# Source turns in halves beside the projections, and score maxima sent in groups, in a transformer block on one core

## The chip, the cores and the metric

The kernel runs on one core of a Trainium2 chip. The metric is the device time of one execution in microseconds (us). TensorE (PE, with its weight loads listed as PEld), VectorE (DVE), ScalarE (ACT) and GpSimd (POOL) compute; SyncE (SP) issues nearly all DMA transfers. Each engine works through its own instructions in order and waits for the others by semaphores.

## The reference

A diffusion-transformer block for 16 batches of 256 tokens, width 256, 16 heads of 16, all in 32-bit floats. What matters here:

```python
x_norm = modulate(_ln(x), shift_a, scale_a)
q, k, v = jnp.split(x_norm @ W_qkv + b_qkv, 3, axis=-1)          # then split into heads
attn_w = softmax(einsum('bhqd,bhkd->bhqk', q, k) * scale)
x = x + gate_a[:, None] * (einsum('bhqk,bhkd->bhqd', attn_w, v) @ W_proj + b_proj)
q_c = _ln(x) @ W_qc + b_qc
k_c, v_c = jnp.split(_ln(context) @ W_kvc + b_kvc, 2, axis=-1)
x = x + cross_attention(q_c, k_c, v_c) @ W_cproj + b_cproj
x = x + gate_m[:, None] * (gelu(modulate(_ln(x), shift_m, scale_m) @ W_mlp1 + b_mlp1) @ W_mlp2 + b_mlp2)
```

## The kernel before

**Units and beats.** The work is a sequence of 32 units, numbered n: the self-attention ("s") and the cross-attention ("c") of each batch. The first five are s units, then s and c alternate, and the last five are c units. After a prologue (n = −1) each unit is worked on in eight beats, k = 0 to 7, by `beat(n, k)`; the MLP of all batches follows. A unit has 16 heads in eight pairs, and four groups g of two pairs.

In beat k of unit n, PE does three kinds of work:

- `visit` computes the scores s of unit n+1 (query rows on partitions) for half t of the tokens of group k // 2: four matmuls into the tile `s` (two PSUM banks, one copy; `s_tile`), two on rows 0 to 63 and two on rows 64 to 127. VectorE reduces them to maxima (tile `mx`, one reduction per beat). It then computes the scores of unit n once more, transposed (`st`, `t_part`), for pair k, and ScalarE takes their exponential into `pt` (`exp`). The transposed scores have the maxima subtracted already, because row 63 of each half of the q operand (`u.q[63:P:64]`) holds minus the maximum and the matching row of k holds ones.
- In even beats `av_part` multiplies the exponentials with the values (tile `o`, in four column tiles of 32).
- In odd beats two *lanes* run side by side, one on rows 0 to 63 and one on rows 64 to 127 (`lane`, `lanes`, `run`): twelve pairs of matmuls for two of the projections Q, K, V (of units n+2 and n+3) and P (of unit n−2). A lane's product is summed over two visits, one half of the rows in each. Beat 1: Q and V; beat 3: P and Q; beat 5: K and P; beat 7: V and K. Where the unit n+3 is a c unit, two lane pairs of beat 5 run between s and st; where n > 1, the first lane pair of beat 7 runs in beat 6.

**Turns of the sources.** A projection's source is the layer-normed input `xn` (128 tokens by 256, twice), turned by PE with an identity into PSUM (`transposed.turn`: four turns of 128 × 128, tile `psT`), then copied out as a high and a low part (`high` on ScalarE, `low` on VectorE, or `full` and `rest_pool`). `T[0]` of unit n+3 is turned half in beat 0 and half in beat 2 of unit n, if it is ready; a c unit has a second source `T[1]`, turned in beat 4.

**The maxima** of a unit are turned in two halves of two groups each (`m_turn`, 16 columns), scaled by −1 on ScalarE (`m_row`, tile `m`) and copied by one DMA into row 63: groups 0 and 1 of unit n+1 in beat 4 of unit n, groups 2 and 3 in beat 0 of the unit itself. In beat 4 the turned maxima borrow a bank of `st` where n+3 is a c unit, and in beat 0 a part of the turned source's bank.

**PSUM.** `st` and `s` take two banks each, the LONG tag one (values and P), and the SHORT tag has three, shared by the tiles `ps_q`/`ps_qc`, `ps_k`/`ps_kc`, `psT`, `psm` and `o`. A new tile takes one of the three banks that has come free and its first writer waits for the last reader of the tile before. The last readers are: for Q and K the low part on VectorE (`l_q` in beat 4, `l_k` in beat 0 of the next unit, both after that beat's reduction), for `o` the copy to `oT` on ScalarE (beat 5, and beat 0 of the next unit), for a turned source its low part (or the copy `y_c`) in beat 3, for `T[1]` its low part in beat 7.

**Order.** The program order on each engine is that of the calls (`tc.keep_in_program_order`). In beat 0 that is: K's high part on ScalarE, s, st, exponential, `o` of the unit before and its copy, turns, maxima, K's low part. Helper calls are all listed at line 51.

Of the kernel before, what the change touches and what calls it, by code (L numbers as in the profile page):

```python
# [21 lines left out]
def pixart_block(  # L22
# [354 lines left out]
    def transposed(src, name, scale=None, pool=False):  # L377
# [6 lines left out]
        def turn(fs=range(KC)):  # L384
            if len(fs) == KC:
                place()
            for f in fs:
                for t in range(NT):
                    PE.transpose(o.ps[:, f * N + t * P:f * N + (t + 1) * P],
                                 src()[:, t, f * P:(f + 1) * P], ident)  # L390

        def high():
# [78 lines left out]
    def lanes(x, y):  # L471


        if x:
            x.ps, x.fresh = ps_gen(f"ps_{x.name}", LONG if x.tok else SHORT), True
        return zip_longest(*(lane(o, half) for half, o in enumerate((x, y)) if o))

# [4 lines left out]
    def to_stack(W, src, bias, dst, which, name):  # L482
# [24 lines left out]
        def low():  # L507
# [3 lines left out]
            if name == "k0":  # L511
                gap(work, 192, "gap_mx")
            for f in range(KC):
# [65 lines left out]
    def build_pre(u):  # L579

        b = u.b
        u.mx = None
        if u.kind == "s":
# [111 lines left out]
    turn_of_s = [0]  # L695

    def s_tile(u, g, par, t, bank=None, home=sp):

# [7 lines left out]
        for j in range(2):  # L706
# [3 lines left out]
            if j == 0:  # L710
                yield
        if u.mx is None:
            u.mx = work.tile([P, 2, 2, 4, NT], F32, tag="mx", name=f"mx_{u.n}", bufs=3)
        mx = u.mx.rearrange("p f r a t -> p r f a t")
        a = slice(2 * (g % 2), 2 * (g % 2) + 2)
        if alone or apart:
            src = home[bank] if apart else sp[:, bank]
            DVE.tensor_reduce(mx[:, par, g // 2, a, t], src.rearrange("p (j n) -> p j n", j=2),
                              AX.X, ALU.max)
# [8 lines left out]
    def m_turn(u, hf, pst=None):  # L728

        if pst is None:  # L730
            pst = ps_gen(f"psm_{u.n}_{hf}", SHORT)
        PE.transpose(pst[:16, :P], u.mx[:, hf].rearrange("p r a t -> p (r a t)"), ident)
        return pst

    def m_row(u, hf, pst):

        m = work.tile([16, P], F32R, tag="m", name=f"m_{u.n}_{hf}", bufs=1)
        ACT.mul(m, pst[:16, :P], -1.0)
        SP.dma_start(u.q[63:P:64, 4 * hf:4 * hf + 4, :].bitcast(F32), m.bitcast(F32))

# [23 lines left out]

    def in_turn(*pieces):

        for _ in range(2):
            for f in pieces:
                next(f)

    def av_part(u, g):

        if g % 2 == 0:
            u.po = ps_gen(f"o_{u.n}_{g}", SHORT).rearrange("p (g n) -> p g n", g=2)
        for c in range(NT):
            for h in range(4):
# [301 lines left out]

    def visit(n, k, home=sp, between=None):

# [8 lines left out]
        t = [t_part(units[n], k, par) for par in range(2)]  # L1089
        in_turn(*s)  # L1090
        if between:
            between()
        in_turn(*t)
        later.append(lambda: exp(units[n], k))

    def spare(n, gate=True):
# [6 lines left out]
    def beat(n, k):  # L1103
# [20 lines left out]
        if k == 6:  # L1124
            if q2 and not n:
                q2.V.keep()
            if p2 and not alone:
                p2.end()
        kp = None
        if k == 5 and lx and n:  # L1130
            kp = lanes(q3.K, None if alone else p2)
        visit(n, k, between=kp and (lambda: run(kp, 2)))
        if k == 0:
            exps()
            if prev:
# [17 lines left out]
        elif k == 1:  # L1153
            exps()
            run(lanes(q2 and q2.Q, q2 and n and q2.V))
            if prev:
# [8 lines left out]
        elif k == 2:  # L1165
            exps()
            if cur:
                av_part(cur, 0)
            if q3:
                q3.T[0].turn((1,) if q3.ready else (0, 1))  # L1170
            if ls:
# [26 lines left out]
        elif k == 4:  # L1198
# [20 lines left out]
        elif k == 5:  # L1219
            exps()  # L1220
            run(kp or lanes(q3 and q3.K, (None if alone else p2) if n else q2.V))
            if cur:
# [10 lines left out]
        elif k == 6:  # L1233
# [139 lines left out]
```

## Time and profile before

| | |
|---|---|
| median of 3 runs | 719.96 us (719.1 to 720.77) |
| profiled execution, from its first to its last instruction | 719.7 us |
| PE busy | 710.4 us (99%), 8993 matmuls |
| DVE busy | 567.8 us (79%), 895 instructions |
| ACT busy | 551.7 us (77%), 955 instructions |
| POOL busy | 520.6 us (72%), 518 instructions |
| reductions of the maxima (units −1 to 30) | start from 21.4 us on (the four into `st` from 19.4), the last at 519.1 us |

An instruction is listed as `out<-in`, by the program's tile names without buffer numbers, with its shape. A busy PE isn't PE at its peak: matmuls are pipelined and their ends are modelled, so a wait of its weight loads may lie under a matmul that is still listed as running. In a timeline, the columns are start, duration (both in us), engine, line, operation, output and inputs, shape and count; a bracket tells how long the engine was idle before it and what ended that.

### The profile page before, as it was taken

Reading aid. Unit: us, or ns where it says so; the run is one execution under the profiler, and the core shown is the slowest. Engines: PE = TensorE matmul, PEld = TensorE weight load, DVE = VectorE, ACT = ScalarE, POOL = GpSimd, SP = SyncE. Lnnn points to the kernel's source line nnn. Section 1 sums busy time; section 2 is a strip of 40 time slices with the busy share of each in tenths; the row PEclk is TensorE's granted clock in tenths of the full one; section 3 lists DMA queues with packets and bytes.
Section 4 is the critical chain, followed back from the end, with each engine's and each line's share of the span. In section 5 each row is a group of like instructions: output and inputs, shape, how many; then the busy total and the mean of one; then the engine's idle time right before and its main releaser. Section 6 shows DMA issues by size and latency. Waiting matters only on the chain.

```text
span 719.7 us, 22488 instructions
## 1 busy us (share of the span) xinstructions
PE 710.4 (99%) x8993; PEld 592.3 (82%) x8993; DVE 567.8 (79%) x895; ACT 551.7 (77%) x955; POOL 520.6 (72%) x518
## 2 busy tenths in 40 slices
PE   9999999999999999999999999999999999999997
PEld 8777777777877778777787777777779999999997
DVE  5878888888888798888888888888675777777653
ACT  5677888888888788887888888887867677666661
POOL 7655778787776867776686798977857988656651
PEclk9999999999999999999999999999999999999999
DMA  7574455554545456454655656456323132313212
GB/s 236 183 233 157 160 170 178 175 179 160 167 151 196 162 176 191 163 166 153 195 167 176 210 174 195 156 192 196 95 78 103 59 87 61 88 46 88 66 39 74
DMA packets 81548, 106.15 MB, mean 147 GB/s; under 512 B 16610, under 2 KB 44548, under 8 KB 81444
## 3 DMA queue, kind: packets, MB, share of 16 engines
q1 hardware_dynamic: 80548, 104.37, 45.5%
q8 instruction: 71, 1.16, 0.7%
q10 hardware_dynamic: 896, 0.35, 0.2%
q14 instruction: 33, 0.27, 0.1%
HBM read 35.89 MB, written 8.98 MB: 62 GB/s over the span
## 4 chain that ended last, share of the span: by engine, by line
PE 94%; DVE 3%; POOL 2%; issue 0%; ACT 0%; POOLq 0%; ACTq 0%
PE s L51 18%; PE o L51 16%; PE st L51 16%; PE ph L51 12%; PE ps_qc L51 4%; PE ps_kc L51 4%; PE ps_k L51 4%; PE ps_q L51 3%; PE ps_v_c L51 3%; PE ps_v_s L51 3%; PE ps_P_s L51 2%; DVE mx L51 2%; PE ps_P_c L51 2%; PE psT_c L51 2%; PE psT_s L51 2%; PE psT_q L51 1%
## 5 line engine op out<-in xcount | busy, mean ns | idle before, releaser
L51 DVE TENSOR_REDUCE mx<-s 128x4 f32<-128x1024 f32 x252 | 307.9, 1222 | 73.5 <-PE s L51 70.1
L51 ACT ACTIVATE pt<-st 128x1024 f32<-128x1024 f32 x256 | 263.4, 1029 | 51.8 <-PE st L51 51.0
L51 PE MATMUL o<-pt,v 128*32 128x256 f32 x2048 | 137.1, 385 | 0.0
L51 PE MATMUL s<-big 63*128 63x256 f32 x1008 | 116.8, 305 | 1.7 <-DVE st_q L51 0.8
L51 PE MATMUL st<-big 64*128 64x256 f32 (+1 forms) x1040 | 107.7, 282 | 0.8 <-issue 0.4
L51 PE MATMUL ph<-xTh_m,wself 128*128 128x256 f32 x512 | 100.2, 281 | 0.0
L51 POOL TENSOR_TENSOR hl<-hf,hh 128x512 fp32r<-128x512 f32 x60 | 80.1, 1350 | 20.8 <-ACT hh L51 20.8
L51 PEld LDWEIGHTS s<-big 63*128 63x128 f32 x1008 | 77.3, 185 | 21.0 <-issue 7.1
L51 PEld LDWEIGHTS o<-pt,v 128*32 128x32 f32 x2048 | 53.4, 109 | 39.5 <-ACT oT L51 1.3
L51 PEld LDWEIGHTS st<-big 64*128 64x128 f32 (+1 forms) x1040 | 81.2, 186 | 3.6 <-ACT pt L51 1.5
L51 PEld LDWEIGHTS ph<-xTh_m,wself 128*128 128x128 f32 x512 | 82.3, 188 | 1.2 <-issue 0.4
L51 PE MATMUL ph<-xTl_m,wself 128*128 128x256 f32 x256 | 71.1, 278 | 0.0
L51 ACT ACTIVATE hf<-ph,bT 128x256 f32<-128x256 f32 x112 | 47.0, 473 | 22.1 <-PE ph L51 21.9
L51 ACT ACTIVATE hh<-ph,bT 128x256 fp32r<-128x256 f32 x112 | 47.0, 472 | 19.8 <-PE st L51 8.4
L51 PEld LDWEIGHTS ph<-xTl_m,wself 128*128 128x128 f32 x256 | 48.2, 188 | 0.0
L51 PE MATMUL s<-big,hh 128*128 128x256 f32 x256 | 45.6, 278 | 0.0
L51 DVE TENSOR_SCALAR xn_m<-x,mv_m,rs_m 128x256 f32<-128x256 f32 x28 | 33.5, 1237 | 14.8 <-POOL rs_m L51 14.8
L51 POOL TENSOR_SCALAR xn_q<-x,mv_q,rs_q 128x256 f32<-128x256 f32 x32 | 38.9, 1225 | 1.7
L51 POOL TENSOR_SCALAR xn_c<-c,mv_c,rs_c 128x256 f32<-128x256 f32 x32 | 38.9, 1226 | 1.7
L51 PE MATMUL st<-big,hh 128*128 128x256 f32 x224 | 40.0, 278 | 0.0
L51 PEld LDWEIGHTS s<-big,hh 128*128 128x128 f32 x256 | 38.8, 188 | 0.0
L51 POOL TENSOR_SCALAR rs_c<-mv_c 128x2 f32<-128x2 f32 x16 | 3.6, 228 | 48.3 <-DVE mv_c L51 48.2
(230 smaller groups left out, 2133.1 us busy)
## 6 DMA issues: line engine op xcount, KB each, us to landing
big<-h_k SPq DMA_DIRECT2D x32, 256.0 KB
big<-h_kc SPq DMA_DIRECT2D x32, 256.0 KB
big<-h_qc SPq DMA_DIRECT2D x32, 256.0 KB
big<-h_q SPq DMA_DIRECT2D x30, 256.0 KB
big<-l_k SPq DMA_DIRECT2D x16, 256.0 KB
g<-gd SPq DMA_DIRECT2D x16, 256.0 KB
U_s<-oT SPq DMA_DIRECT2D x32, 128.0 KB
R_s<-rd_s SPq DMA_DIRECT2D x16, 256.0 KB
```

The costliest lines, as they stand in the source:

```text
L51: i = f(*a, **k)
```

## The change

The turn of a source is split into two halves by rows (`half(h)`: rows 64h to 64h + 63, four turns of 64 × 128 into 64 columns each). In beat 1 (`T[0]` of unit n+3, if ready) and beat 5 (`T[1]`, for c units) a new PSUM tile is taken for the source after that of Q or K, and the first half runs between the first and the second pair of the score matmuls (`mid`), mixed with two matmuls of the second lane in the order t, b, t, t, b, t (`turning`). The lanes of that beat then run ten pairs, and the last two matmuls of the first lane run in the next beat (2 or 6), between s and st, mixed with the second half of the turn. The turns of beats 0, 2 and 4 go, as do the two lane pairs between s and st in beat 5. Where n+3 is a c unit, the lane pair of beat 6 goes back to beat 7.

The maxima have a constant tile of four places (`mxs`), each with two groups of eight columns. In beat 2, ahead of the matmuls of `o`, one place is turned by two plain matmuls with the identity in column tiles of 32 (`m_cols`): group 3 of unit n and group 0 of unit n+1. In beat 6 another follows: groups 1 and 2 of unit n+1. They are written to the free half of the bank of `o`, scaled on ScalarE and sent by four DMAs (`m_send`). The turns of the maxima in beats 0 and 4 go (but for unit 0).

```diff
+    mxs = const.tile([P, 4, 32], F32, name="mxs")
+    POOL.memset(mxs, 0.0)
+    mxs = [mxs[:, i] for i in range(4)]
...
+        def half(h):
+            rows = slice(64 * h, 64 * h + 64)
+            for f in range(KC):
+                for t in range(NT):
+                    c = f * N + t * P + 64 * h
+                    PE.transpose(o.ps[:, c:c + 64], src()[rows, t, f * P:(f + 1) * P], ident[rows, rows])
+                    yield
...
+    def turning(T, h, beside):
+        t = T.half(h)
+        for f in (t, beside, t, t, beside, t):
+            next(f)
...
+    def place_of_max(u, g):
+        w, i = (2 + g // 2, g % 2) if u.n == 0 else (2 + u.n % 2, g - 1) if g in (1, 2) else ((u.n - (g == 0)) % 2, g == 0)
+        return mxs[w][:, 8 * i:8 * i + 8].rearrange("p (r a t) -> p r a t", r=2, t=NT)
...
-            DVE.tensor_reduce(mx[:, :, g // 2, a, t], home.rearrange("p r (j n) -> p r j n", j=2),
+            DVE.tensor_reduce(mx[:, :, :, t], home.rearrange("p r (j n) -> p r j n", j=2),
...
+    def m_cols(w, pst):
+        for j in range(2):
+            PE.matmul(pst[32 * j:32 * j + 32, :64], w, ident[:, 64 * j:64 * j + 64], start=True, stop=True,
+                      tile_position=(0, 32 * j))
+
+    def m_send(pst, *parts):
+        m = work.tile([64, 64], F32R, tag="m2", name="m2", bufs=1)
+        ACT.mul(m, pst[:64, :64], -1.0)
+        for u, g, row in parts:
+            for j in range(2):
+                to = u.q[63:P:64, 2 * g:2 * g + 2].rearrange("r a (t q) -> r a t q", t=NT)[..., 64 * j:64 * j + 64]
+                SP.dma_start(to.bitcast(F32), m[32 * j + row:32 * j + row + 8].bitcast(F32))
...
-    def in_turn(*pieces):
-
-        for _ in range(2):
+    def in_turn(*pieces, mid=None):
+
+        for i in range(2):
             for f in pieces:
                 next(f)
-
-    def av_part(u, g):
+            if mid and not i:
+                mid()
...
-        kp = None
-        if k == 5 and lx and n:
-            kp = lanes(q3.K, None if alone else p2)
-        visit(n, k, between=kp and (lambda: run(kp, 2)))
+        between, mid = None, None
+        if k in (1, 5):
+            x, y, T = ((q2 and q2.Q, q2 and n and q2.V, q3 and q3.ready and q3.T[0]) if k == 1 else
+                       (q3 and q3.K, (None if alone else p2) if n else q2.V, lx and lx.T[1]))
+            if x:
+                x.ps, x.fresh = ps_gen(f"ps_{x.name}", LONG if x.tok else SHORT), True
+            a, b = pair_of(x, y)
+            steps = weave(a, b)
+            if T:
+                T.place()
+                held.append((T, a))
+                mid = lambda: turning(T, 0, b)
+        elif held:
+            between = lambda: turning(held[0][0], 1, held.pop()[1])
+        visit(n, k, between=between, mid=mid)
+        def rest_of():
+            run(steps, 10 if held else 12)
         if k == 0:
             exps()
+            if n == 0:
+                m_part(cur, 1)
             if prev:
                 av_part(prev, 3)
-            if q3 and q3.ready:
-                q3.T[0].place()
-                pst = m_turn(cur, 1, q3.T[0].ps[:, N:])
-                q3.T[0].turn((0,))
-            else:
-                pst = m_turn(cur, 1)
-            if prev:
                 p1.pull_sums(1)
-            m_row(cur, 1, pst)
...
             if cur:
-                av_part(cur, 0)
-            if q3:
-                q3.T[0].turn((1,) if q3.ready else (0, 1))
+                parts = [(cur, 3, 0)] * (n > 0) + [(nxt, 0, 8)] * bool(nxt)
+                av_part(cur, 0, mxs[n % 2])
+                m_send(cur.po[:, 1], *parts)
+            if q3 and not q3.ready:
+                q3.T[0].turn()
...
-            if lx:
-                lx.T[1].turn()
-            if nxt:
-                m_part(nxt, 0, st[:, 0] if lx else None)
...
-                av_part(cur, 2)
+                av_part(cur, 2, nxt and mxs[2 + nxt.n % 2])
+                if nxt:
+                    m_send(cur.po[:, 1], (nxt, 1, 0), (nxt, 2, 8))
                 cur.post.pull(0)
             if q3 and p2:
                 q3.vk = lanes(q3.V, q3.K)
-                run(q3.vk, 1)
+                run(q3.vk, 0 if lx else 1)
```

More of the change, by code (lines that the diff above doesn't have):

```diff
@@ L390, in turn @@
                                  src()[:, t, f * P:(f + 1) * P], ident)
+        def half(h):
[5 more added lines that the diff above has]
+                    yield
+        o.half = half
         def high():
@@ L475, in lanes, with pair_of, weave @@
             x.ps, x.fresh = ps_gen(f"ps_{x.name}", LONG if x.tok else SHORT), True
-        return zip_longest(*(lane(o, half) for half, o in enumerate((x, y)) if o))
+        return weave(*pair_of(x, y))
+    def pair_of(x, y):
+        return [lane(o, half) if o else iter(()) for half, o in enumerate((x, y))]
+    def weave(*gens):
+        return zip_longest(*gens)
+    def turning(T, h, beside):
+        t = T.half(h)
+        for f in (t, beside, t, t, beside, t):
+            next(f)
     def run(steps, n=12):
@@ L511, in low @@
             if name == "k0":
-                gap(work, 192, "gap_mx")
+                gap(work, 576, "gap_mx")
             for f in range(KC):
@@ L711, in s_tile @@
                 yield
[L712 to L715, printed above, removed]
+        mx = place_of_max(u, g)
         if alone or apart:
             src = home[bank] if apart else sp[:, bank]
-            DVE.tensor_reduce(mx[:, par, g // 2, a, t], src.rearrange("p (j n) -> p j n", j=2),
+            DVE.tensor_reduce(mx[:, par, :, t], src.rearrange("p (j n) -> p j n", j=2),
                               AX.X, ALU.max)
         elif bank == 1:
-            DVE.tensor_reduce(mx[:, :, g // 2, a, t], home.rearrange("p r (j n) -> p r j n", j=2),
+            DVE.tensor_reduce(mx[:, :, :, t], home.rearrange("p r (j n) -> p r j n", j=2),
                               AX.X, ALU.max)
@@ L731, in m_turn @@
             pst = ps_gen(f"psm_{u.n}_{hf}", SHORT)
-        PE.transpose(pst[:16, :P], u.mx[:, hf].rearrange("p r a t -> p (r a t)"), ident)
+        PE.transpose(pst[:16, :P], mxs[2 + hf][:, :16], ident)
         return pst
+    def m_cols(w, pst):
[9 more added lines that the diff above has]
+                SP.dma_start(to.bitcast(F32), m[32 * j + row:32 * j + row + 8].bitcast(F32))
     def m_row(u, hf, pst):
@@ L738, in m_row @@
         ACT.mul(m, pst[:16, :P], -1.0)
-        SP.dma_start(u.q[63:P:64, 4 * hf:4 * hf + 4, :].bitcast(F32), m.bitcast(F32))
+        for g in range(2):
+            a = 4 * hf + 2 * g
+            SP.dma_start(u.q[63:P:64, a:a + 2].bitcast(F32), m[8 * g:8 * g + 8].bitcast(F32))
     def t_part(u, pair, par):
@@ L763, in exps, with av_part @@
         later.clear()
-    def in_turn(*pieces):
-        for _ in range(2):
+    def in_turn(*pieces, mid=None):
+        for i in range(2):
             for f in pieces:
                 next(f)
-    def av_part(u, g):
+            if mid and not i:
+                mid()
+    def av_part(u, g, w=None):
         if g % 2 == 0:
             u.po = ps_gen(f"o_{u.n}_{g}", SHORT).rearrange("p (g n) -> p g n", g=2)
+            if w is not None:
+                m_cols(w, u.po[:, 1])
         for c in range(NT):
@@ L1077, in unit, with visit @@
         return units[n] if 0 <= n < nu else None
-    def visit(n, k, home=sp, between=None):
+    def visit(n, k, home=sp, between=None, mid=None):
         v, e = unit(n + 1), k
@@ L1094, in visit @@
         later.append(lambda: exp(units[n], k))
+    held = []
     def spare(n, gate=True):
@@ L1154, in beat @@
             exps()
-            run(lanes(q2 and q2.Q, q2 and n and q2.V))
+            rest_of()
             if prev:
@@ L1220, in beat @@
             exps()
-            run(kp or lanes(q3 and q3.K, (None if alone else p2) if n else q2.V))
+            rest_of()
             if cur:
```

3 lines of the change are left out of this document (1 added, 2 removed).

## The prediction

> **What bounds the kernel now.** I read the page's first part and the chain, then the waits, then the timelines of VectorE (DVE) and of the matmuls (PE) over units 16 and 17 (284 to 315 us). Page rows, the costliest VectorE group, and one row of the waits:
>
> ```profile
> span 719.7 us, 22488 instructions
> PE 710.4 (99%) x8993; PEld 592.3 (82%) x8993; DVE 567.8 (79%) x895; ACT 551.7 (77%) x955; POOL 520.6 (72%) x518
> PE 94%; DVE 3%; POOL 2%; issue 0%; ACT 0%; POOLq 0%; ACTq 0%
> L51 DVE TENSOR_REDUCE mx<-s 128x4 f32<-128x1024 f32 x252 | 307.9, 1222 | 73.5 <-PE s L51 70.1
> PEld s L51 <- DVE mx L51: 5.4, 14, 0.6
> ```
>
> PE looks like the only bound. But the last row says that weight loads of the scores s already wait for the maxima: s has one place in PSUM, so the scores of a beat can't start before the reduction of the beat before has read it. I call the reductions of a unit's beats R0 to R7. VectorE, first a unit of one turned source ("short", unit 16), then one of two ("long", unit 17, to R0 of the next); columns start, duration, instruction:
>
> ```profile
> 284.03 1.23 DVE L51 TENSOR_REDUCE mx<-s 128x4 f32<-128x1024 f32 x1
> 285.17 0.87 DVE L51 SCALAR_TENSOR_TENSOR l_kc<-ps_kc,bP,h_kc 128x256 fp32r<-128x256 f32 x2
> 286.14 1.23 DVE L51 TENSOR_REDUCE mx<-s 128x4 f32<-128x1024 f32 x1
> 287.28 0.74 DVE L51 BATCH_NORM_STATS2 st_c<-c 128x6 f32<-128x256 f32 x2
> 288.02 1.23 DVE L51 TENSOR_REDUCE mx<-s 128x4 f32<-128x1024 f32 x1
> ...
> 290.07 1.23 DVE L51 TENSOR_REDUCE mx<-s 128x4 f32<-128x1024 f32 x1 [0.56 <-PE s L51]
> ...
> 295.72 1.22 DVE L51 TENSOR_REDUCE mx<-s 128x4 f32<-128x1024 f32 x1 [0.45 <-PE s L51]
> 297.55 1.22 DVE L51 TENSOR_REDUCE mx<-s 128x4 f32<-128x1024 f32 x1 [0.60 <-PE s L51]
> ...
> 299.38 1.23 DVE L51 TENSOR_REDUCE mx<-s 128x4 f32<-128x1024 f32 x1
> 300.52 0.87 DVE L51 SCALAR_TENSOR_TENSOR l_k<-ps_k,bqkv,h_k 128x256 fp32r<-128x256 f32 x2
> 301.48 1.23 DVE L51 TENSOR_REDUCE mx<-s 128x4 f32<-128x1024 f32 x1
> ...
> 303.40 1.23 DVE L51 TENSOR_REDUCE mx<-s 128x4 f32<-128x1024 f32 x1 [0.55 <-PE s L51]
> ...
> 305.44 1.23 DVE L51 TENSOR_REDUCE mx<-s 128x4 f32<-128x1024 f32 x1 [0.15 <-PE s L51]
> ...
> 307.31 1.23 DVE L51 TENSOR_REDUCE mx<-s 128x4 f32<-128x1024 f32 x1 [0.39 <-PE s L51]
> 308.45 0.87 DVE L51 SCALAR_TENSOR_TENSOR l_q<-ps_q,bqkv,h_q 128x256 fp32r<-128x256 f32 x2
> 309.24 0.24 DVE L51 BATCH_NORM_AGGREGATE mv_s<-st_s 128x2 f32<-128x6 f32 x2
> 309.70 1.22 DVE L51 TENSOR_REDUCE mx<-s 128x4 f32<-128x1024 f32 x1 [0.23 <-PE s L51]
> 311.56 1.23 DVE L51 TENSOR_REDUCE mx<-s 128x4 f32<-128x1024 f32 x1 [0.63 <-PE s L51]
> 313.40 1.23 DVE L51 TENSOR_REDUCE mx<-s 128x4 f32<-128x1024 f32 x1 [0.61 <-PE s L51]
> ...
> 315.23 1.22 DVE L51 TENSOR_REDUCE mx<-s 128x4 f32<-128x1024 f32 x1
> ```
>
> The short unit takes 15.35 us from R0 to R0, the long one 15.85. PE, the load that opens Q's lane, and the copy of the attention output, same unit:
>
> ```profile
> 300.71 0.60 ACT L51 COPY oT<-o 128x512 f32<-128x512 f32 x1
> 300.93 0.51 PE L51 MATMUL s<-big 63*128 63x256 f32 x4
> 301.27 0.41 PE L51 MATMUL st<-big 64*128 64x256 f32 x4
> 301.44 0.18 PEld L51 LDWEIGHTS ps_q<-xTh_s,wself 64*128 64x128 f32 x1
> 301.51 0.32 PE L51 MATMUL ps_q<-xTh_s,wself 64*128 64x256 f32 x1
> 301.52 0.31 PE L51 MATMUL ps_v_s<-wself,xTh_s 64*128 64x256 f32 x1
> ...
> 302.84 0.28 PE L51 MATMUL ps_q<-xTl_s,wself 64*128 64x256 f32 x1
> 302.93 0.43 PE L51 MATMUL s<-big 63*128 63x256 f32 x4
> 303.17 0.42 PE L51 MATMUL st<-big 64*128 64x256 f32 x4
> 303.52 1.07 PE L51 MATMUL o<-pt,v 128*32 128x256 f32 x16
> 304.53 0.44 PE L51 MATMUL psT_c<-ident,xn_c 128*128 128x128 f32 x2
> 304.90 0.50 PE L51 MATMUL s<-big 63*128 63x256 f32 x4
> 308.43 0.66 PE L51 MATMUL psT_q<-ident,xn_q 128*128 128x128 f32 x4
> ```
>
> From these: s to its reduction is 0.55 us after o (300.93, 301.48) and 0.47 after lanes (302.93, 303.40). l_k ends at 301.39 and Q's load starts at 301.44: it waited for the bank that l_k had read, so VectorE to PE is 0.05. A reduction thus can't follow the last sooner than 1.23 + 0.05 + 0.55 = 1.83 (odd beats) or 1.75 (even beats). R6 to R7 and R7 to R0 are 1.83 to 1.84 already: part of PE's 99% hides no slack, and PE time taken off pays only down to these floors.
>
> **The change part by part.** *The turns leave beats 0, 2 and 4 and run as eight half turns beside two lane matmuls.* A whole turn costs PE (0.66 − 0.44)/2 = 0.11 (four against two); a half streams 64 of 128 columns, an estimate of 0.055. Four of them take 0.22, the two lane matmuls beside them on the other rows 2 × 0.12 (twelve pairs, 301.51 to 302.93). So I price one stretch (t, b, t, t, b, t) at 0.22, if both row halves run at once as ps_q and ps_v_s do (starts 0.01 apart); one after the other it would be 4 × 0.11 + 2 × 0.12 = 0.68. I take 0.22: the pair is the nearest row. The two stretches of a turn take up two of the lanes' twelve pairs, so ten are left.
>
> *The first stretch stands between the halves of s, and its bank is new.* The three short PSUM banks go round: a tile takes the bank that came free longest ago and waits for its last reader. In beat 1 two are wanted: Q takes the older, the turn is left with K's (free after l_k) or the attention output's (free after oT). Before, the turn was placed in beat 0 on an old bank and Q waited, after st, by 0.05 only. Now the turn waits in front of the second half of s, and PE issues in order: lanes, st and the reduction queue behind it. l_k ends 2.01 after R0 in both units (284.03 to 286.04; 299.38 to 301.39); oT ends at 301.31 and, behind the exponential, would be no earlier relative to a shorter beat 0. So R0 to R1 = 2.01 + 0.05 + stretch 0.22 + 0.33 (second pair of s to the reduction: 0.55 less the first pair, 0.34 − 0.12) = 2.61. Same in beat 5 of a long unit: K takes the old turn's bank, the second turn gets Q's, free after l_q, which ends 307.31 to 309.32, 2.01 again: R4 to R5 = 2.61.
>
> *Beat by beat, after against before.* Short unit: R0–R1 2.61 for 2.11, +0.50. R1–R2 unchanged: reduction and st_c follow each other without a gap. R2–R3: the beat on PE is 0.59 (s to o) + 1.01 (o) + 0.22 + 0.06 (maxima, 64 columns) = 1.88, the floor 1.83, and R2 comes late in its beat: 1.83 for 2.05, −0.22. R6–R7: the maxima add 0.05. The rest is unchanged: +0.33. Long unit: R0–R1 2.61 for 2.10, +0.51. R1–R2 floor 1.75 for 1.92, −0.17 (ten pairs need less). R2–R3 1.88 − 0.47 + 0.55 = 1.96 for 2.04, −0.08. R4–R5 2.61 for 2.39, +0.22; that beat loses 0.66 of turns and a maxima turn, and the wait eats it. R5–R6 1.75 for 1.86, −0.11. R6–R7 1.96 for 1.84, +0.12 (stretch and maxima for one lane pair). R7–R0: twelve pairs, not eleven, and s after o: 1.92 as R1–R2 was, for 1.83, +0.09. Sum +0.58.
>
> *Maxima in groups.* Two turns of 0.11 go, two of 0.055 in column tiles come; counted above. The scaling on ScalarE stays two per unit, now behind the exponentials of beats 2 and 6; only DMAs read it, and ScalarE is at 77%, so I cost it at nothing. The row copies grow from two to eight DMAs:
>
> ```profile
> L51 SPq DMA_DIRECT2D big<-m x64: 557/577/630, 28.9 to 523.7; - x64
> ```
>
> Six more of about 0.6 are 3.6 us on SP's queue per 16 us unit. Four now stand ahead of the pulls of beat 6, delaying those, K's sends and the sums S by up to 2.5. The rows themselves are wanted a beat pair later or more. The one close reader is the reciprocal after R2 of a short unit: nothing to 0.3 us, at most 12 × 0.3 = 4 us; I take nothing, since longer beats give it back.
>
> *Sum.* The first turn is halved in units 1 to 28: 12 short (1, 2, 4 to 22 even) and 16 long (3 to 23 odd, 24 to 28). 12 × 0.33 + 16 × 0.58 = 13.2. The profiled execution spans 719.7, 0.3 under the median of 719.96: 719.96 + 13.2 = 733.
>
> The Trainium skill (TensorE: Matmul & The Clock Gate, section on 56 ns and 53.3 ns) says that with hardware decode off the sequencer spends about 62 ns on each matmul, which then binds short ones. By it a stretch of six takes 0.37 and the sum would be about 746. The two lane starts 0.01 apart speak against it here.
>
> **The rivals.** *No wait (faster).* If the turn finds a free bank, R0–R1 is floor plus stretch, 2.05; R4–R5 is 2.17, since VectorE ends l_q and mv_s at 309.48. Short −0.06 − 0.22 + 0.05 = −0.23, long 0.58 − 0.56 − 0.44 = −0.42: 12 × −0.23 + 16 × −0.42 = −9.5, 710. It decides where the bank's last reader ends before the first pair of s does, 0.22 into the beat; against it, l_k starts only when R0 is done, and so does s. *Only the first wait*: if K takes Q's bank and the second turn the old one, long is 0.58 − 0.44 = +0.14: 12 × 0.33 + 16 × 0.14 = +6, 726. *Paced by issue*: lanes run 24 matmuls in 1.42, 0.059 each; if that is the sequencer, a stretch is 0.355, 88 stretches × 0.135 = +12: 745. *Halves one after another*, so the change doesn't do what it says: 88 × 0.46 = +40: 773. For it: no row shows a turn on half the rows.
>
> **How the numbers follow.** Forecast 733: 0.68; first wait only 0.08; no wait 0.13; issue 0.05; serial 0.06. Range 717 to 747: it leaves out no wait and serial, 0.19; its ends allow 14 us for errors of 0.1 in the beats. A measurement can tell 0.2%, 1.4 us: faster 0.14 (no wait and a little of the first case), same 0.03, slower 0.83.
>
> **What would show it.** Right: first turns of psT in beats 1 and 5 starting 0.05 after l_k or l_q (or oT), waits of PE loads of psT for VectorE or ScalarE of over 0.4 us some 44 times, R0–R1 near 2.6, and PE's share below 99%. Wrong: psT loads without a wait and R0–R1 near 2.05 (no wait); psT and lane matmuls starting 0.1 apart (serial); reciprocals that wait for S.

## The result, and the profile after

The changed kernel takes 724.04 us (median of 6 runs, 722.41 to 726.45), the kernel before 719.53 us (6 runs, 717.56 to 720.77) beside it: ratio 1.0068, 95% interval 1.0044 to 1.0092. It is slower, as forecast, but by 4.5 us and not by 13. Its profiled execution took 722.92 us. From the page of the changed kernel, and its waits:

```profile
span 721.1 us, 23569 instructions
PE 704.2 (98%) x9359; PEld 600.5 (83%) x9359; DVE 566.5 (79%) x895; ACT 551.0 (76%) x956; POOL 520.5 (72%) x519
PE 75%; DVE 13%; DMA 4%; issue 2%; POOL 2%; SPq 2%; ACT 1%; POOLq 0%; ACTq 0%; DVEq 0%
PEld s L51 <- DVE mxs L51: 62.3, 122, 1.2
DVE S_s L51 <- DMA S_s<-oT: 8.0, 10, 2.0
DVE S_c L51 <- DMA S_c<-oT: 3.7, 3, 2.0
DVE st_s L51 <- DMA x<-in_x_dram: 3.6, 5, 1.6
```

PE has 6.2 us less to do (710.4 before), but its share of the chain fell from 94% to 75%, with VectorE at 13% and DMAs at 4%. The loads of the scores s now wait for the maxima's reduction 122 times (62.3 us; before 14 times, 5.4). And waits for DMAs have come: 11.7 us of the reciprocal for the sums S (0.6 before), 3.6 of the statistics for x (1.4 before). The columns of the waits are total, times and longest.

VectorE in units 20 (one turned source) and 21 (two), where no beat is lengthened by a DMA; R0 of unit 20 is the first row, R0 of unit 21 the last but one, R0 of unit 22 the last:

```profile
349.75 1.22 DVE L51 TENSOR_REDUCE mxs<-s 128x4 f32<-128x1024 f32 x1
...
351.88 1.23 DVE L51 TENSOR_REDUCE mxs<-s 128x4 f32<-128x1024 f32 x1
...
353.71 1.22 DVE L51 TENSOR_REDUCE mxs<-s 128x4 f32<-128x1024 f32 x1
355.51 0.35 DVE L51 RECIPROCAL S_s<-S_s 128x32 f32<-128x32 f32 x1 [0.57 <-DMA S_s<-oT]
355.78 1.22 DVE L51 TENSOR_REDUCE mxs<-s 128x4 f32<-128x1024 f32 x1
...
365.16 1.22 DVE L51 TENSOR_REDUCE mxs<-s 128x4 f32<-128x1024 f32 x1
...
380.99 1.23 DVE L51 TENSOR_REDUCE mxs<-s 128x4 f32<-128x1024 f32 x1
```

A short unit takes 15.41 us, a long one 15.83: nearly as before (15.35 and 15.85 in the prediction's units 16 and 17). So the loss isn't in every unit. It is in single beats, and the largest is this one (unit 18: R2, the late reciprocal, R3; then SP's queue):

```profile
320.94 1.22 DVE L51 TENSOR_REDUCE mxs<-s 128x4 f32<-128x1024 f32 x1
324.12 0.35 DVE L51 RECIPROCAL S_s<-S_s 128x32 f32<-128x32 f32 x1 [1.95 <-DMA S_s<-oT]
324.39 1.16 DVE L51 TENSOR_REDUCE mxs<-s 128x4 f32<-128x1024 f32 x1
```

```profile
315.27 2.23 SPq L51 DMA_DIRECT2D big<-m  x4
...
319.51 2.64 SPq L51 DMA_DIRECT2D big<-h_kc  x2
322.24 0.60 SPq L51 DMA_DIRECT2D S_s<-oT  x1
```

Four row DMAs hold SP for 2.23 us, K's sends follow late, and the second part of S is issued at 322.24. The reciprocal stands ahead of the next reduction on VectorE, that reduction ahead of the next scores on PE: 3.45 us from R2 to R3, which are 2.07 apart in unit 20 (355.78 − 353.71).

The rows are not the whole of this beat. K's two sends took 2.64 us here, and 1.22 in unit 20:

```profile
352.24 1.22 SPq L51 DMA_DIRECT2D big<-h_kc  x2
353.55 0.60 SPq L51 DMA_DIRECT2D S_s<-oT  x1
```

R2–R3 is longer than its median by 0.9 us in units 14 and 16 and by 1.4 in unit 18, and these three are the short units with long K sends (2.24, 2.15 and 2.64 us). The kernel before has such sends too, 2.12 us in unit 10 and 2.02 in unit 16, and they cost nothing there. In the changed kernel no slack is left for them: even in unit 20 the reciprocal waits 0.57 us for S and ends (355.86) when the next reduction could start (355.78). From the issue of S to the reciprocal it is 1.88 us in unit 18 and 1.96 in unit 20, so the landing is no slower; the issue is late. Why single sends take longer is not known. With units 15 and 17 (0.4 each), this beat loses 4 us.

The wait that the forecast rested on isn't there. Beat 1 of unit 17 on PE, then the load that opens Q's lane and the low part of K:

```profile
302.16 0.39 PE L51 MATMUL s<-big 63*128 63x256 f32 x2
302.38 0.22 PE L51 MATMUL psT_c<-ident,xn_c 64*128 64x64 f32 x1
302.39 0.27 PE L51 MATMUL ps_v_s<-wself,xTh_s 64*128 64x256 f32 x1
302.44 0.28 PE L51 MATMUL psT_c<-ident,xn_c 64*128 64x64 f32 x2
302.50 0.28 PE L51 MATMUL ps_v_s<-wself,xTh_s 64*128 64x256 f32 x1
302.56 0.22 PE L51 MATMUL psT_c<-ident,xn_c 64*128 64x64 f32 x1
302.60 0.36 PE L51 MATMUL s<-big 63*128 63x256 f32 x2
```

```profile
302.94 0.18 PEld L51 LDWEIGHTS ps_q<-xTh_s,wself 64*128 64x128 f32 x1
```

```profile
302.02 0.87 DVE L51 SCALAR_TENSOR_TENSOR l_k<-ps_k,bqkv,h_k 128x256 fp32r<-128x256 f32 x2
```

The first turn runs at 302.38, in the middle of l_k (302.02 to 302.89); it is Q's load that starts 0.05 after l_k. So the turn took the old free bank and Q the one of l_k: Q's first write stands behind st, the turn's ahead of it.

### The profile page after: what moved, and what is told of

It is laid out like the page before. It is cut to its first block, busy times and chain, and to the rows that moved or that the text cites. A ratio compares the mean times of both kernels' runs of the same rounds, so it can differ in the third digit from the quotient of the medians.

```text
span 721.1 us, 23569 instructions
## 1 busy us (share of the span) xinstructions
PE 704.2 (98%) x9359; PEld 600.5 (83%) x9359; DVE 566.5 (79%) x895; ACT 551.0 (76%) x956; POOL 520.5 (72%) x519
## 4 chain that ended last, share of the span: by engine, by line
PE 75%; DVE 13%; DMA 4%; issue 2%; POOL 2%; SPq 2%; ACT 1%; POOLq 0%; ACTq 0%; DVEq 0%
PE s L51 18%; PE st L51 13%; PE ph L51 12%; PE o L51 10%; DVE mxs L51 9%; PE ps_kc L51 3%; PE ps_q L51 3%; PE ps_P_s L51 2%; PE ps_k L51 2%; PE ps_v_c L51 2%; SPq L51 2%; PE ps_qc L51 2%; DMA x<-in_x_dram 2%; PE ps_v_s L51 1%; DMA U_s<-oT 1%
## 5 line engine op out<-in xcount | busy, mean ns | idle before, releaser
L51 DVE TENSOR_REDUCE mxs<-s 128x4 f32<-128x1024 f32 x252 | 307.6, 1221 | 65.3 <-PE s L51 60.0
L51 PE MATMUL s<-big 63*128 63x256 f32 x1008 | 132.9, 322 | 10.9 <-DVE mxs L51 4.3
L51 PE MATMUL o<-pt,v 128*32 128x256 f32 x2048 | 141.6, 384 | 0.0
L51 PEld LDWEIGHTS s<-big 63*128 63x128 f32 x1008 | 82.4, 185 | 70.4 <-DVE mxs L51 62.3
L51 PE MATMUL st<-big 64*128 64x256 f32 (+1 forms) x1040 | 112.4, 285 | 0.3 <-ACT pt L51 0.2
L51 PEld LDWEIGHTS st<-big 64*128 64x128 f32 (+1 forms) x1040 | 85.7, 186 | 3.0 <-ACT pt L51 1.4
L51 PEld LDWEIGHTS o<-pt,v 128*32 128x32 f32 x2048 | 67.0, 109 | 21.7
L51 POOL TENSOR_SCALAR rs_c<-mv_c 128x2 f32<-128x2 f32 x16 | 3.6, 228 | 53.5 <-DVE mv_c L51 53.3
```

What stands on the lines that cost most here:

```text
L51: i = f(*a, **k)
```

## The experiments

Ratios are to the kernel before, measured beside each on the same chip. Medians of beats are over units 1 to 28, counted on PE from the first score matmul of one beat to that of the next; medians of units go from R0 to R0.

**Half of the rows.** The second DMA of each pair goes, so half of the maxima's rows are not sent.

```diff
-            for j in range(2):
+            for j in range(1):
                 to = u.q[63:P:64, ...]
```

> The changed kernel without the second DMA of each pair that carries maxima: half of the maxima's rows are left out, so 4 row DMAs per unit stand in SP's queue instead of 8; nothing else is changed. Theory A (the rows delay SP's queue, so the sums S land late and the reciprocal on VectorE, and the reduction behind it, wait for them in beat 3): the stalls of 0.2 to 1.2 us in beat 3 of units 14 to 18 go, the waits of the reciprocal on S in the waits view fall from 13 to a few, and the time falls by 3 to 4.5 us against the changed kernel, to a ratio of 0.999 to 1.003 against the kernel before. Theory B (the loss is PE work that the two lanes' turns make longer, given back in beats 1, 2, 5 and 6): the time stays within 1 us of the changed kernel, ratio 1.005 to 1.009.

718.76 us, 0.999 (0.9974 to 1.0005): 0.8% of the time, over 5 us, came off with the DMAs alone. The waits:

```profile
DVE S_c L51 <- DMA S_c<-oT: 1.6, 2, 1.0
DVE S_s L51 <- DMA S_s<-oT: 1.0, 2, 0.8
```

11.7 us of waits on S have become 2.6, and the median lengths of the beats are those of the changed kernel. Theory A holds: the change's net loss is in SP's queue.

**Six row DMAs.**

```diff
-                    m_send(cur.po[:, 1], (nxt, 1, 0), (nxt, 2, 8))       # 4 DMAs of 8 rows
+                    m_send(cur.po[:, 1], (nxt, 1, 0, 2))                 # 2 DMAs of 16 rows
...
```

> The changed kernel with the columns of groups 1 and 2 side by side, so that each DMA of beat 6 takes 16 rows: 6 row DMAs per unit in place of 8, nothing left out, nothing else changed. SP's busy share in the units (DMA issues, 100 to 500 us) was 0.60 before, 0.79 in the changed kernel, 0.68 with 4 row DMAs; here some 0.74. Theory A (each row DMA delays the queue of SP): about half of the 5 us that came off with 4 row DMAs, ratio 1.001 to 1.006, and the waits of the reciprocal on S between 11.7 us (changed) and 1.6 us (4 row DMAs). Rival (a threshold: the queue only hurts when it is nearly full): all of it, ratio 0.997 to 1.001.

719.59 us, 0.9999 (0.9983 to 1.0015): better than theory A's half, the rival's range. All rows are sent, and the waits on S are down to 2.0 us. Two of eight DMAs carry nearly the whole loss.

**Four row DMAs by whole transposes.**

```diff
-        for j in range(2):
-            PE.matmul(pst[32 * j:32 * j + 32, :64], w, ident[:, 64 * j:64 * j + 64], ...)
+        PE.transpose(pst[:16, :P], w[:, :16], ident)
...
```

> The changed kernel with the 16 columns of maxima transposed by one matmul of 128 rows and sent as 2 DMAs of 8 rows by 128 in place of 4 of 8 by 64: 4 row DMAs per unit in place of 8, all rows are sent; PE has one matmul of 128 columns in place of two of 64 beside each other (0 to 0.06 us more, twice per unit). Theory A (SP's queue): the stalls of beat 3 go as in the run that leaves half of the rows out, the time falls by 2.5 to 4.5 us against the changed kernel, ratio 0.999 to 1.004. Theory B (the turns' own PE time): the same time or up to 1.5 us more than the changed kernel, ratio 1.006 to 1.010.

725.85 us, 1.0096 (1.0076 to 1.0116). Theory A's time wasn't met, but its mechanism shows: the reciprocal's waits on S are 1.6 us, and in their place beat 2, and beat 6 of the long units, took 2.18 us by the median, not 2.07 (beat 6 of the short units 2.04, not 1.94). Twice 0.11 in 28 units is 6 us: a transpose of 128 rows costs PE 0.11 us more than two matmuls of 64 in column tiles. I had allowed 0.06.

**Eight row DMAs in the kernel before.**

```diff
-        SP.dma_start(u.q[63:P:64, 4 * hf:4 * hf + 4, :].bitcast(F32), m.bitcast(F32))
+        for j in range(2):
+            for a in range(4 * hf, 4 * hf + 4, 2):
+                r = 2 * (a % 4) + 8 * j
+                SP.dma_start(u.q[63 + 64 * j:64 + 64 * j, a:a + 2, :].bitcast(F32), m[r:r + 4].bitcast(F32))
```

> The kernel before with each of its row DMAs (16 rows of 128) split into 4 of 4 rows: 8 row DMAs of 2 KB per unit as in the changed kernel, sent in beats 0 and 4 as before; nothing else is changed, PE's work is that of the kernel before. Theory A (the count in SP's queue is what costs): stalls of single beats as in the changed kernel, 3 to 6 us more, ratio 1.003 to 1.009. Rival (it is the place of the rows, just ahead of S in the queue, and not their count): in beat 0 they stand behind S here, so ratio 0.998 to 1.002.

742.33 us, 1.0328 (1.0297 to 1.0359): both expectations too low. SP's queue in unit 21, and the reduction that opens unit 22:

```profile
389.73 2.56 SPq L51 DMA_DIRECT2D big<-m  x4
392.38 0.59 SPq L51 DMA_DIRECT2D big<-l_q  x1
```

```profile
397.24 1.22 DVE L51 TENSOR_REDUCE mx<-s 128x4 f32<-128x1024 f32 x1 [1.83 <-PE s L51]
```

The rows of beat 4 stand ahead of Q's low part, which the first scores in unit 22 read, and those come 1.83 us late. The waits view doesn't name that DMA here. For it speaks that in most units these scores' loads start 1.8 to 2.2 us after its issue has ended, where the kernel before mostly leaves 3.8 to 4.0; in unit 21 it is 3.7, so there the landing was late as well. By the traces 18 of the 20 us between the two profiled spans (739.5 and 719.7) lie in such ends of beat 7. Both count and place decide: eight DMAs cost 23 us where four stand ahead of Q, and 5 us where they stand ahead of S.

**Other DMAs moved from SP to POOL**: in the kernel before, in the changed kernel, and in the run with six rows and half of the turns whole (below).

```diff
-        SP.dma_start(X[b], tok(x, b))
+        (POOL if b > 4 else SP).dma_start(X[b], tok(x, b))
...
-            SP.dma_start(u.ct, tok(ctxt, u.b))
+            POOL.dma_start(u.ct, tok(ctxt, u.b))
...
-                SP.dma_start(tok(X2d, b), o.out)
+                POOL.dma_start(tok(X2d, b), o.out)
```

> The kernel before with the same 43 loads and stores issued by POOL in place of SP. SP's queue is busy 0.60 of the time there and the waits view shows next to no waits on its DMAs, so all that is to be had is the few stalls of single beats: ratio 0.997 to 1.001. If POOL's issues cost its own work: 1.002 to 1.008, and then the runs with the changed kernel carry the same cost.

> The changed kernel, 8 row DMAs per unit, with the same 43 loads and stores issued by POOL in place of SP. Theory A (SP's queue as a whole): its issues go from about 22 to about 20.5 per unit, a fourth of the way to the run with 4 row DMAs, so 1 to 2.5 us less than the changed kernel, ratio 1.002 to 1.005. If the rows' DMAs hurt by themselves (engines, landings) and not through the queue: the time of the changed kernel, 1.006 to 1.009.

> The run with 6 row DMAs and the first half of the features turned whole, and the DMAs that nothing waits for soon (x of the units behind the fifth, the context, the store of the cross units' rows: 43 in all) issued by POOL in place of SP. In that run nearly all units were at 15.31 (one turned source) and 15.80 us (two), below the kernel before (15.35, 15.89), and single beats of units 0, 23, 24 and 28 were 0.7 to 2.3 us longer, because Q and the rows came late out of SP's queue. If SP's queue is the cause: these stalls become rare, 717 to 719 us, ratio 0.996 to 1.000. If POOL's issues delay its own work (it is busy 72% of the span) or the late landings come from the DMA engines and not from the queue: 721 us or more, ratio 1.002 to 1.010.

726.03 (1.0099, 1.0072 to 1.0126), 727.98 (1.0115, 1.0094 to 1.0137) and 727.64 us (1.0107, 1.0083 to 1.0131), each above the higher of its expectations. The 43 DMAs cost the kernel before 6.4 us, and POOL 32.6 us of busy time (553.2 for 520.6), 0.76 each. The trace of the first shows where much of the 6.4 is:

```profile
135.69 0.75 DVE L51 BATCH_NORM_STATS2 st_c<-c 128x6 f32<-128x256 f32 x2 [3.06 <-DMA c<-in_ctx_dram]
```

POOL issues this context load between its own instructions, 1.1 us after R0 of unit 6 (130.37 and 129.31), where SP had issued it 2.9 us ahead of R0 (123.93 and 126.80). The statistics wait 4.1, 3.9 and 4.5 us for the context in the three runs, and not at all in the kernel before and the changed kernel. So something did wait for these DMAs soon. In the changed kernel the waits on S fall only from 11.7 to 9.6 us; the runs say nothing more of SP's queue. The Trainium skill (Perfetto Trace Analysis, section DMA Optimizations) says that balancing DMAs over sync, scalar and GPSIMD may help where descriptor generation is the bottleneck; here it did not. The same section advises batching small transfers into larger ones (2 KB into 4 KB or 8 KB, for example), for the sake of bandwidth; the six rows batch 2 KB into 4 KB, and what they gain here is issue time on SP.

**The forecast's wait, made on purpose.** A matmul of 2 columns makes Q or K the first writer.

```diff
+                PE.matmul(x.ps[:, :2], wz[:64, :P], wz[:64, :2], start=True, stop=True)
                 T.place()
```

> The changed kernel with one matmul of 2 columns ahead of each turned source, into the bank of Q or K, which the lanes write over later: by that Q or K is the bank's first writer and takes the bank that is free, and the turn takes the bank that the low part still reads on VectorE. This makes the wait that the forecast had put into the change. If the forecast's price of the wait was right and only its place in the order of banks was wrong: beats 1 and 5 go from 2.13 to about 2.6 to 2.7 us in each of the 44 places (12 in the units with one turned source, 32 in those with two), the time to 740 to 750, ratio 1.028 to 1.042. If the wait is hidden or short even then (the scores behind it wait for the reduction anyway): below 728, ratio under 1.011.

750.75 us, 1.0445 (1.0423 to 1.0467), just above the upper end. VectorE in one beat 1, and the turn's load:

```profile
314.74 1.23 DVE L51 TENSOR_REDUCE mxs<-s 128x4 f32<-128x1024 f32 x1
315.88 0.87 DVE L51 SCALAR_TENSOR_TENSOR l_k<-ps_k,bqkv,h_k 128x256 fp32r<-128x256 f32 x2
317.56 1.22 DVE L51 TENSOR_REDUCE mxs<-s 128x4 f32<-128x1024 f32 x1 [0.81 <-PE s L51]
```

```profile
316.86 0.14 PEld L51 LDWEIGHTS psT_c<-ident,xn_c 64*128 64x128 f32 x1 [0.60 <-issue]
```

The turn's load starts 0.11 after l_k, and R0–R1 is 2.82 us where the forecast had 2.61 and the changed kernel has 2.13. The mechanism was priced 0.2 us too low per place; it belongs to an order of banks that this kernel doesn't have.

**The maxima alone**, with the turns of before.

```diff
-            if T:
-                T.place()
-                held.append((T, a))
-                mid = lambda: turning(T, 0, b)
...
+            if q3 and q3.ready:
+                q3.T[0].place()
+                q3.T[0].turn((0,))
...
```

> The maxima in groups as in the changed kernel (8 row DMAs per unit, transposed ahead of the values of beats 2 and 6), the turns of the sources as in the kernel before (T[0] in beats 0 and 2, T[1] in beat 4, whole 128-wide). Theory A (SP's queue): the stalls of beat 3 are there as in the changed kernel; some 0.1 us per unit of PE work is saved in beats 0 and 4 and nothing is lost in beats 1 and 5, so ratio 1.001 to 1.006. Theory B (the turns are the loss): the time is that of the kernel before or below it, ratio 0.996 to 1.000, and beats 1, 2, 5, 6 have their old lengths (2.0, 1.96 us).

729.71 us, 1.0138 (1.0115 to 1.016): slower than the changed kernel, which neither theory expected. R0 of units 20, 21 and 22:

```profile
348.91 1.23 DVE L51 TENSOR_REDUCE mxs<-s 128x4 f32<-128x1024 f32 x1
...
364.44 1.23 DVE L51 TENSOR_REDUCE mxs<-s 128x4 f32<-128x1024 f32 x1
...
380.52 1.23 DVE L51 TENSOR_REDUCE mxs<-s 128x4 f32<-128x1024 f32 x1
```

15.53 and 16.08 us, 0.1 and 0.25 over the changed kernel. By the medians, beats 2 and 6 grew by about 0.09 and 0.11 to 0.15 against before and beat 1 by 0.06, while beat 0 gave back 0.03; what beat 4 of the long units gave (0.13), beat 5 took. Waits on S are there too (11.4 us). So the maxima cost about 10 us, some 6 of them in the beats of every unit (15.55 and 16.10 by the median, 15.37 and 15.86 before), and beside them the turns gain about 5.

**The turns alone, in four forms.** First with the maxima as before, in the bank of the next turn; second the same with the first half of the features turned whole (the last two lines).

```diff
             if q3 and q3.ready:
                 q3.T[0].place()
                 pst = m_turn(cur, 1, q3.T[0].ps[:, N:])
-                q3.T[0].turn((0,))
             else:
                 pst = m_turn(cur, 1)
+            if q3 and q3.ready:
+                q3.T[0].turn((0,))
...
```

> The turns of the sources in halves as in the changed kernel, the maxima as in the kernel before (two transposes of 16 columns per unit, in beats 0 and 4, into the bank of the source that is turned next; 2 row DMAs per unit). Theory A (the turns gain, the maxima lose: the run with the maxima alone was 10 us slower than before, the changed kernel 5): no stalls on S, beats 2 and 6 lose the 0.06 to 0.11 us of the columns of maxima, beats 0 and 4 take the transpose under the floor that the reduction sets: 0.1 to 0.2 us less per unit than the run with 4 row DMAs (15.34 and 15.86), so 712 to 716 us, ratio 0.990 to 0.996. Rival (the transpose of the maxima in beats 0 and 4 is on the path there as well): ratio 0.998 to 1.004.

> The run with the turns alone (maxima as before), and of each turned source the first half of the features transposed whole in beat 0 or 4, the second half in halves by the lanes. Beats 0 and 4 hold the transpose of the maxima here already (0.1 us), so the 0.22 of the two whole transposes costs 0.1 to 0.2 there, and the shorter stretches give back 0.1 to 0.15 in each of beats 1, 2, 5, 6: between 5 us less and the same as the run with the turns alone, ratio 0.985 to 0.996.

740.93 us (1.0301, 1.0277 to 1.0325) and 736.77 us (1.0248, 1.0221 to 1.0275). Both far off, and the trace of the first says why: ScalarE's scaling of the maxima, and the first row of the turn:

```profile
311.90 0.26 ACT L51 ACTIVATE m<-psT_c 16x128 fp32r<-16x128 f32 x1
```

```profile
312.31 0.24 PE L51 MATMUL psT_c<-ident,xn_c 64*128 64x64 f32 x1 [0.50 <-POOL xTh_as L51]
```

```profile
PE psT_s L51 <- ACT m L51: 6.5, 12, 0.6
PE psT_c L51 <- ACT m L51: 5.6, 11, 0.6
```

The scaling ends at 312.16 and the turn begins 0.15 later, in the same bank and ahead of the second pair of s; the waits name it 23 times, though the bracket names another releaser here. That is the forecast's kind of wait, from another reader. The next two forms put the scaling ahead of the values and the copy of o; the third has the half-whole turns, and in beat 4 the scaling behind them.

```diff
-            if prev:
-                av_part(prev, 3)
...
+            m_row(cur, 1, pst)
             if prev:
+                av_part(prev, 3)
                 p1.pull_sums(1)
-            m_row(cur, 1, pst)
```

> The run with the turns alone and the first half of the features turned whole, with ScalarE's multiplication of the maxima put ahead of what made it late: in beat 0 the maxima are transposed and multiplied ahead of the values and of the copy of o, in beat 4 of the long units the whole transposes are issued ahead of the multiplication. Theory A (the turns gain by themselves, and the two runs with the turns alone were slow only because the turn of beat 1 or 5 waited for that multiplication: it ended at 312.17 and the turn began at 312.31, 0.14 later, in unit after unit): no such wait is left, beats 1 and 5 at 2.0, 0.16 us less per turned source than with whole turns, so 712 to 717 us, ratio 0.990 to 0.997. Rival (the turn waits for something else in that bank, or the gain of the turns was never theirs): ratio 1.005 or more.

> The first run with the turns alone (all 8 half turns of a source by the lanes), with the multiplication of the maxima of beat 0 ahead of the copy of o; beat 4 of the long units is unchanged. Theory A: the wait of beat 1 goes (0.4 us in each unit), that of beat 5 shortens by little, since the multiplication there stands right behind the exponential; 740.9 us falls by 8 to 12 us, and what is left over the run above shows what the wait in beat 5 costs. Rival: no change, 738 us or more.

721.24 us (1.002, 1.0001 to 1.0039) and 729.25 us (1.0132, 1.0111 to 1.0153): 15.5 and 11.7 us better than the same turns without the edit. That shows the scaling to be the cause of most of the loss, though the third form fell between its two expectations. No trace of the fourth form is read. In the third, short units were at 15.26 us by the median (15.37 before) and long ones at 16.01 (15.86), where a wait is left in each of the 16:

```profile
PEld psT_q L51 <- ACT m L51: 4.9, 16, 0.6
```

The last expectation below counts the same units on PE, from scores to scores, which gives it slightly other numbers.

**Six rows and half-whole turns.** In the run with six row DMAs, two whole transposes in beat 0 or 4, and two half turns beside one lane matmul in place of four beside two.

```diff
-        for f in (t, beside, t, t, beside, t):
+        for f in (t, beside, t):
...
```

> The run with 6 row DMAs per unit, and of each turned source the first half of the features transposed whole (two 128-wide transposes) at the end of beat 0 or 4, where the reduction sets the end, and only the second half of the features turned in halves by the lanes (2 turns beside 1 lane matmul in place of 4 beside 2). If beats 0 and 4 have the slack that the floor promises (PE work 1.6 us under a floor of 1.75 to 1.82, so 0.22 more costs 0 to 0.1 there) and the shorter stretches give 0.1 to 0.15 back in each of beats 1, 2, 5, 6: 4 to 9 us less than the run with 6 row DMAs, ratio 0.990 to 0.997. If beats 0 and 4 grow by the whole 0.22: within 2 us of it.

722.6 us, 1.0042 (1.0022 to 1.0061): 3 us more than six rows alone, which neither case expected. Beats 0 and 4 have no slack: by the medians they grew by 0.21 to 0.23, and each beat with a shortened stretch lost 0.12. R0 and R1 of unit 20, 2.23 us apart for 2.13 in the changed kernel:

```profile
346.20 1.23 DVE L51 TENSOR_REDUCE mxs<-s 128x4 f32<-128x1024 f32 x1
...
348.43 1.23 DVE L51 TENSOR_REDUCE mxs<-s 128x4 f32<-128x1024 f32 x1 [0.22 <-PE s L51]
```

One lane pair more runs in beat 1 than in the changed kernel, and yet the beat is shorter on PE, since the reduction comes 0.73 us after s by the medians, not 0.85. So in the changed kernel's beat 1 PE waits for a reduction that its own stretch has delayed. Typical units are at 15.37 and 15.77 us, but single beats of units 0, 23, 24 and 28 lose 0.7 to 2.3 us more than with six rows alone (in an execution of 726.17 us, 3.6 above this run's median).

**One source's turn alone.** The third form for `T[0]` only; `T[1]` and beats 4 to 7 as before.

> The kernel before with one part of the change: only T[0], the source that every unit has, is turned in part by the lanes (first half of its features whole in beat 0, second half in halves in beats 1 and 2), with the maxima's multiplication of beat 0 ahead of the values; T[1] of the long units and the maxima of beat 4 stay as before. In the run before this one the short units had 15.17 us against 15.35 before, the long ones 16.02 against 15.89, where the turn of T[1] in beat 5 waited 0.34 us for the multiplication of the maxima; their beats 0 to 2 were 0.10 us shorter. If the gain of T[0] stands without T[1]: 12 times 0.18 and 16 times 0.10, 3 to 4.5 us less than before, ratio 0.994 to 0.997. If the long units lose it in beats 4 and 5 again: ratio 0.998 to 1.001.

717.77 us (12 runs) against 719.73 (17 runs): 0.9977 (0.9962 to 0.9991), faster than both kernels, by little. The chain from its page, and R0 of units 20, 21 and 22:

```profile
PE 95%; DVE 4%; issue 0%; ACT 0%; POOL 0%; ACTq 0%; POOLq 0%
```

```profile
344.54 1.22 DVE L51 TENSOR_REDUCE mx<-s 128x4 f32<-128x1024 f32 x1
...
359.83 1.22 DVE L51 TENSOR_REDUCE mx<-s 128x4 f32<-128x1024 f32 x1
...
375.58 1.23 DVE L51 TENSOR_REDUCE mx<-s 128x4 f32<-128x1024 f32 x1
```

15.29 and 15.75 us, and PE carries the chain again. The gain is 2 us, some half of what was expected: 0.05 and 0.13 us in these two units (15.34 and 15.88 before).

A form with the first half turns behind both pairs of s, which wouldn't delay the reduction, was not tried, so what the place of the stretch costs by itself is not shown.

## Why the prediction had the sign but not the mechanism or the size

- **The bank (the step that failed).** "Q takes the older, the turn is left with K's" took the order in which the tiles are named. Banks go in the order of the first write, and the turn's comes ahead of Q's. The first rival, no wait, was the real case. The forced wait shows that its price would have been 27 us against the changed kernel (forecast: 2.61 for R0–R1; measured 2.82).
- **Why the rival's 710 didn't come.** The changed kernel's beats stop at higher floors than I set. R0–R1: 2.05 in the rival, measured 2.13 (351.88 − 349.75); the next point has the reason. R1–R2 in long units: 1.75 forecast, 1.83 by the median, as in odd beats. R2–R3 of a short unit: 1.83 forecast, over PE work of 1.88; measured 2.07, and PE itself takes that long from s to s. Beat 2 of unit 20 on PE:

```profile
353.17 0.50 PE L51 MATMUL s<-big 63*128 63x256 f32 x4
...
353.73 0.48 PE L51 MATMUL st<-big 64*128 64x256 f32 x4
354.14 0.25 PE L51 MATMUL o<-ident,mxs 128*32 128x64 f32 x2
...
355.24 0.50 PE L51 MATMUL s<-big 63*128 63x256 f32 x4
```

  From s to st it is 0.56: the stretch's 0.22 and 0.34, where 0.24 was counted. From st to o it is 0.41 for 0.35, and from there to the next s 1.10 for 1.07: 2.07 in place of 1.88. The 0.34 has a likely reason: a PE that stands waiting for the reduction has no weights loaded ahead, so what follows s comes 0.10 later. That would explain R1–R2 and half of R2–R3; it was not tried apart, and the other 0.09 of R2–R3 is only measured. So of −0.23 and −0.42 per unit about nothing was left, 9 us over the 28 units.
- **The stretch.** 0.22 was right: 302.38 to 302.60. But the first turn starts 0.22 after the first pair of s, where the second pair had followed after 0.12; with that, the second pair comes 0.32 later (302.60 − 302.16 − 0.12), and s to its reduction is 0.85 us, not 0.77. One after another (0.68) is refuted: turn and lane start 0.01 apart. The Trainium skill (TensorE: Matmul & The Clock Gate, section on 56 ns and 53.3 ns) has 62 ns per matmul with hardware decode off, by which, as an estimate, six would take 0.37. The trace has 0.22 for six, so that bound doesn't act here.
- **The maxima.** "Two turns of 0.11 go, two of 0.055 come" was a gain on paper; alone they cost 10 us. What goes lies in beats 0 and 4, what comes in beats 2 and 6.
- **SP's queue.** Costed at nothing, "since longer beats give it back", with a bound of 4 us. Without the long beats it cost about 5, by the reader named, the reciprocal, and by x, a load further back in the same queue, which I had not looked at. The single long K sends, which the queue no longer absorbs, I had not looked at either.
- **The starting point.** The prediction took the profiled execution of the kernel before for one 0.3 us under the median. In the changed kernel the time is 1.8 us more than the span (722.92 for 721.1); by that, as an estimate, the 719.7 belongs to an execution of 721.5, above the median. The sum starts from the median, so it is not changed.

The prediction's signs of being wrong came in the bank and in the queue: turns without a wait (with R0–R1 at 2.13, not 2.05) and reciprocals that wait for S. So 724 lies inside 717 to 747 by two errors that cancel in part: without the wait the same steps gave 710, and the floors (9 us) and SP's queue (5 us), both priced too low, make it 724. That the sign came out right is luck.

Open: why single K sends take 2 us, and why single beats of units 24 and 28 are hit by six rows and half-whole turns and not by six rows alone (units 0 and 23 lose 0.9 us with six rows too).

## What to carry to other kernels

Before a wait for a buffer is priced, find which instruction writes each new tile first, in the order of the engine: that decides who inherits the busy buffer, and a multiplication or copy still reading it stops all that the waiting engine has behind. Count the DMAs of a queue in issue time and look at which transfer stands behind the added ones; here two small DMAs fewer per unit took back nearly the whole 4.5 us. A queue that just fits has nothing left for a single long transfer, and a load moved to a busy engine is issued when that engine gets to it. PE work pays only where PE ends the beat, so a stretch put ahead of what the next engine waits for can cost on the critical path what it saves in busy time.

## What was not expected of the hardware

A turn on half the rows and a lane matmul on the other half start 0.01 us apart (302.38 and 302.39), and half turns follow each other every 0.06 (302.38, 302.44, 302.56 with one between). Two matmuls of 64 columns in different column tiles are 0.11 us cheaper than one transpose of 128 rows, per send. A row DMA holds SP as long with 16 rows as with 8 (in the run with six, two of 16 rows took 1.15 us, four of 8 rows 2.29), so the count is the price, not the bytes. Single sends of K that usually hold SP for 0.6 us took 1.5 to 2.0 in units 14, 16 and 18.
